# A fused transformer block on one core: statistics of the first band groups in fours, an earlier turn, fewer held banks, later statistics

## The chip, the cores and the metric

The kernel runs on one core of a Trainium2 chip. The metric is device time in microseconds (us), from one launch to its end, as the median of several runs. A core has five engines that run side by side and wait for each other with semaphores: TensorE (PE) for matrix products, VectorE (DVE), ScalarE (ACT), GpSimd (POOL), and SyncE (SP), which here issues most of the transfers between the core's memory (SBUF) and the device memory. PE writes its products into PSUM, which has eight banks of 512 float32 per partition.

## The reference

The input `x` is [2, 256, 128, 128]: batch, time, frequency, channel. All is float32. Three residual parts follow each other:

```python
xt = _ln(x, ln_t_w, ln_t_b).transpose(0, 2, 1, 3)
x = x + _mha(xt, t_wi, t_bi, t_wo, t_bo, H_T, cm).transpose(0, 2, 1, 3)
xf = _ln(x, ln_f_w, ln_f_b)
x = x + _mha(xf, f_wi, f_bi, f_wo, f_bo, H_F, bm)
xn = _ln(x, ln_n_w, ln_n_b)
h = jax.nn.gelu(xn @ w1.T + b1, approximate=False)
x = x + (h @ w2.T + b2)
```

`_ln` subtracts the mean over the channels and divides by the root of the variance plus 1e-5. `_mha` is attention with four heads of 32 channels: over the 256 times with a causal mask `cm` first, then over the 128 frequencies with a mask `bm` that keeps 16 neighbours on each side.

## The kernel before

**Groups.** The work is cut into groups of 512 rows (four tiles of 128). There are 128 groups of attention over time (`OverTime`, groups 0 to 127). Then come 16 runs; each has eight groups of attention over frequencies (`OverBands`) and eight of the feed-forward part (`FeedForward`) on the same rows. The first run's band groups are groups 128 to 135.

**A group's way.** `load` fetches `x`. `statistics` (DVE) takes mean and variance of each row into `mv`: four `bn_stats`, four `bn_aggr`. The reciprocal root of the variance, `rstd`, comes either from `root` on GpSimd (an addition and a power), or from ACT (`root_by_scalar`, logarithm and exponential) with a Newton step of three small DVE instructions (`refine`). `normalize` (DVE) writes `xh`; `turn` transposes blocks of it into `z` (DVE) and sends `z` through device memory with four DMAs into `turned`; `fetch` brings it back transposed as `xnT`. PE then makes queries and keys (`queries_keys`), values (`values`), scores, row sums (`rp`, a product with ones) and weighted values (`op`) in `weigh`. ACT takes the exponentials; GpSimd masks them (`first_mask`), except those of the last band head, to which DVE adds the mask beforehand in PSUM (`by_vector`). ACT's `invert` forms a reciprocal of `rp`; `divide` (DVE) makes three steps: the correction on `rp`, then `u`, then `oT`. `output` (PE) makes `yp`; `finish` (DVE) adds it to the residual and stores it, with four DMAs in every second group. In a feed-forward group PE multiplies by `w1` in four slices (`hidden`), ACT applies GELU, PE multiplies by `w2` (`weigh`), and DVE's `divide` adds the residual.

**The order.** `run` (lines 1111 to 1238) has one loop over steps `n`. Each step does parts of several groups: the scores of group `n`, `weigh` and `divide` of `n-1`, `output` and `finish` of `n-2`, `normalize` and `turn` of `n+3` or `n+4`, queries of `n+1` or `n+2`, statistics further ahead. Every instruction is pinned to the program's order on its engine (`InOrder`), so this loop is the order of each engine's queue, SP's DMAs included; the engines meet only where data or a buffer make one wait.

**Fours.** For groups 12 to 127, four groups share one tile of statistics [128, 16] (`Four`): statistics of group `n+8` in step `n`; after the fourth, `root_in_bank` writes the root of all sixteen columns into a PSUM bank, and one `refine` serves four groups. The first band groups do it alone: `due` places their statistics in steps 123, 124, 124, 125, 127, 128, 129 and 130 and, at the end of the same steps, `root_by_scalar` and `refine`, four columns wide, with the root in SBUF.

**Banks.** In time steps banks have fixed places (`Attention.place`). Elsewhere `turn_of_bank` hands out the eight banks in turn; a bank that comes round again can only be written after its last reader. `OverBands.weigh` takes two turns ahead, `yp` and `qp`, into `held`, for the `output` and `queries_keys` that follow in that step. After the last two band groups of a run no queries follow: one turn is skipped, and the last `qp` is left in `held` and used by the first group of the next run.

"Turn" (in the code, `turn`) is also the name of the first feed-forward step of a run, in which `invert_exactly` uses DVE's reciprocal because ACT has already loaded the table for GELU.

The places that the change touches, in the loop:

```python
do_at(n + 3, (OverBands, FeedForward), "normalize", "turn")
do_at(n + 4, OverTime, "normalize")
if old is not None:
    do(n - 2, "finish")
do_at(n + 4, OverTime, "turn")
...
do_at(n + 5, FeedForward, "statistics")
...
do(n - 1, "weigh")
...
if bands[2] or turn:
    do(n - 2, "output", "finish")
do(n - 1, "divide")
```

All instructions issued through `InOrder` carry one line number in the profile, L926; they are told apart by their tiles. A PSUM tile is always called `bank`.

Of the kernel before, what the change touches and what calls it, by code (L numbers as in the profile page):

```python
# [10 lines left out]
F32 = mybir.dt.float32  # L11
# [8 lines left out]
P = 128  # L20
# [5 lines left out]
NT = 4  # L26
# [399 lines left out]


class Group:

# [22 lines left out]
            vector.bn_aggr(self.mv[:, i, :], stats[:, i, :])  # L454

    def means(self):
        return self.path.small.tile([P, NT, 2], F32, name="mv", bufs=16)

    def root(self):
        path, gpsimd = self.path, self.path.gpsimd  # L460
# [92 lines left out]
    def weigh(self):  # L553
        pass
# [30 lines left out]


class Attention(Group):
    four = None
    which = None
    swapped = ()  # L590
    place = {}
# [77 lines left out]
def rows_of(h):  # L669
    return slice(h * D, (h + 1) * D)  # L670
# [9 lines left out]
class OverTime(Attention):  # L680
# [3 lines left out]
    which = 0  # L684
    swapped = (1, 3)
    early, late = (1, 2), (0, 3)

    def means(self):
        if self.four is None:
            return super().means()  # L690
        if self is self.four.groups[0]:
            self.four.mv = self.path.small.tile([P, NT * NT, 2], F32, name="mvs", bufs=3)
        return self.four.part(self.four.mv, self)

    def values(self):
        path = self.path
# [91 lines left out]
def time_scores(old, new):  # L788


    if new is not None:
        new.first_tiles()
    if old is not None:
        old.second_tiles()
    for kind, h, s, e in TIME_ORDER:
        if kind == "s" and old is not None:
            old.second_scores(int(h), int(s), int(e) * HALF)
        if kind == "f" and new is not None:
            new.first_scores(int(h), int(s), int(e) * HALF)


class OverBands(Attention):


    which = 1
    by_vector = 1

    def scores(self, heads):
# [38 lines left out]
    def weigh(self):  # L847
        path = self.path

        path.held = dict(yp=path.turn_of_bank(), qp=path.turn_of_bank())  # L850
        self.rp = path.bank([P, NT * P], "rp")
        for h in range(H):
            path.tensor.matmul(
                self.rp[rows_of(h), :], path.k.ones[:, 0:D], self.p[:, h].rearrange("p i q -> p (i q)"),
                start=True, stop=True,
            )
        self.op = path.bank([P, NT * P], "op")
        for i in range(NT):
            c = slice(i * P, (i + 1) * P)
            for h in range(H):  # L860
                r = rows_of(h)
                path.tensor.matmul(self.op[r, c], self.v[:, i, r], self.p[:, h, i, :], start=True, stop=True)
# [68 lines left out]
class BoundedPath:  # L931
# [179 lines left out]
    def run(self, x, out):  # L1111
        groups = list(self.groups(x, out))

        def do(n, *names):
            if 0 <= n < len(groups):
                for name in names:
                    getattr(groups[n], name)()

        def at(n, kind):
            return 0 <= n < len(groups) and isinstance(groups[n], kind)  # L1120

        def do_at(n, kind, *names):
            if at(n, kind):
                do(n, *names)


        timed = [g for g in groups if isinstance(g, OverTime)]
        fours = {i + NT - 1: Four(self, timed[i : i + NT]) for i in range(3 * NT, len(timed), NT)}

        run0 = [i for i in range(len(groups)) if at(i, OverBands)][: RUN // NT]  # L1130
        due = dict(zip(run0, (-5, -4, -4, -3, -1, 0, 1, 2)))
        due = {n: [i for i in run0 if run0[0] + due[i] == n] for n in range(-12, len(groups) + 2)}
        A = RUN // NT

        self.scalar.preload_act_table_set(EXP_SET)
        for n in range(-12, len(groups) + 2):
            feeds = [at(n - 2 + i, FeedForward) for i in range(5)]
            bands = [at(n - 2 + i, OverBands) for i in range(5)]
            turn = feeds[2] and bands[1]
            old, new = (groups[i] if at(i, OverTime) else None for i in (n, n + 1))  # L1140
            if bands[2] and feeds[1]:
                self.scalar.preload_act_table_set(EXP_SET)
            do_at(n + 4, FeedForward, "root")
            do(n, "first_half", "first_function", "first_mask")
            if n >= 0:
                if n + 5 < 3 * NT:
                    do(n + 5, "statistics")
                if n >= NT:
                    do_at(n + 2 * NT, OverTime, "statistics")
            if old is not None or new is not None:  # L1150
                time_scores(old, new)
                b = self.banks
                Attention.place = dict(yp=b["b0"], rp=b["b3"], op=b["a1"], qp=b["a2"], kp=b["b1"], vp0=b["b0"], vp1=b["b2"])
            else:
                Attention.place = {}
            if old is not None:
                old.second_weights(old.late)
                do(n - 2, "output")
            if new is not None:
                new.first_weights(new.early[:1])  # L1160
            if old is not None:
                old.second_weights(old.early)
                old.mask_second()
                old.add(0)
                old.add(1)
            if new is not None:
                new.first_weights(new.early[1:])
            if n >= 0:
                if n + 5 < 3 * NT:
                    do(n + 5, "root_in_bank")  # L1170
                if n + 2 * NT in fours:
                    fours[n + 2 * NT].root_in_bank()
            if turn:
                do(n, "second_half", "second_function")
            do_at(n + 3, OverTime, "fetch")
            do_at(n + 2, (OverBands, FeedForward), "fetch")

            for i in (2 * n + 12, 2 * n + 13) if n < 2 else (n + 14,):
                if i >= NT:
                    do(i, "load")  # L1180
            if n < -8:
                do(n + 12, "load")
            if n >= 0:
                for i in due[n]:
                    do(i, "statistics")
            do_at(n + 3, (OverBands, FeedForward), "normalize", "turn")
            do_at(n + 4, OverTime, "normalize")
            if old is not None:
                do(n - 2, "finish")
            do_at(n + 4, OverTime, "turn")  # L1190
            if n >= 0:
                if n + 5 < 3 * NT:
                    do(n + 5, "refine")
                if n + 2 * NT in fours:
                    fours[n + 2 * NT].refine()
            if n < 0:
                do(n + 5, "statistics")
            do_at(n + 5, FeedForward, "statistics")
            if n == -4:
                self.fold_rest()  # L1200
                self.warm()
            do(n - 1, "weigh")
            do(n - 1, "invert_exactly" if turn else "invert")
            if new is not None:
                new.first_weights(new.late)
            if bands[2] or turn:
                do(n - 2, "output", "finish")
            do(n - 1, "divide")
            if not turn:
                do(n, "second_half", "second_function")  # L1210
            if n in run0:
                do(n, "bias")
            if not bands[2] and old is None:
                do_at(n, FeedForward, "bias")
                do_at(n + A, OverBands, "bias")
                if at(n - 1, FeedForward) and at(n - 2, OverBands):
                    do_at(n + A - 1, OverBands, "statistics", "root")
                if not turn:
                    do_at(n + A, OverBands, "statistics", "root")
            do_at(n + 2, OverTime, "queries_keys", "take_query", "take_key")  # L1220
            do_at(n + 1, OverBands, "queries_keys", "take_query", "take_key")
            if n < 0:
                do_at(n + 5, OverTime, "root_by_scalar", "refine")
            for i in due[n]:
                do(i, "root_by_scalar", "refine")
            do_at(n, OverTime, "bias")
            if new is not None:
                new.mask_first()
            if not bands[2] and not turn and old is None:
                do(n - 2, "output", "finish")  # L1230
            do_at(n + 2, OverTime, "values", "take_values")
            do_at(n + 1, OverBands, "values", "take_values")
            if old is not None or new is not None:

                b = self.banks
                self.banks = dict(
                    a1=b["b3"], a2=b["a2"], b0=b["a0"], b3=b["a3"], a0=b["a1"], a3=b["b1"], b1=b["b0"], b2=b["b2"]
                )
# [69 lines left out]
```

## Time and profile before

| | us |
|---|---|
| median of three runs | 2680.13 |
| lowest and highest | 2678.06, 2683.11 |
| profiled execution | 2683.14 |
| its span, first to last instruction | 2681.4 |
| busy: PE, DVE, POOL, ACT | 2638.5, 2146.5, 1950.0, 1844.5 |
| granted PE clock, mean | 0.999 |

The stages in the trace: time groups to about 944 us, then sixteen runs of about 107 us. Busy times in stretches of 50 us show that the engines stand differently in them: from 300 to 350 us PE is busy 50.0 us, DVE 42.3, ACT 45.0, POOL 46.4; from 1300 to 1350, around the band groups of a run, PE 49.2, DVE 49.1, ACT 31.8, POOL 35.7; from 1350 to 1400, mostly feed-forward, PE 50.0, DVE 29.5.

A line of a timeline has the start and length in us, engine, source line, operation, output and input tiles with their shapes, how many such instructions were merged, and, in brackets, how long the engine was idle before and whom it waited for. Ends of PE instructions are modelled, so a busy PE may still be waiting inside a group of matmuls: the distance between the starts of the same product in successive steps tells more.

### The profile page before, as it was taken

Reading aid. Unit: us, or ns where it says so; the run is one execution under the profiler, and the core shown is the slowest. Engines: PE = TensorE matmul, PEld = TensorE weight load, DVE = VectorE, ACT = ScalarE, POOL = GpSimd, SP = SyncE. Lnnn points to the kernel's source line nnn. Section 1 sums busy time; section 2 is a strip of 40 time slices with the busy share of each in tenths; the row PEclk is TensorE's granted clock in tenths of the full one; section 3 lists DMA queues with packets and bytes.
Section 4 is the critical chain, followed back from the end, with each engine's and each line's share of the span. In section 5 each row is a group of like instructions: output and inputs, shape, how many; then the busy total and the mean of one; then the engine's idle time right before and its main releaser. Section 6 shows DMA issues by size and latency. Waiting matters only on the chain.

```text
span 2681.4 us, 156498 instructions
## 1 busy us (share of the span) xinstructions
PE 2638.5 (98%) x68662; PEld 1805.6 (67%) x68662; DVE 2146.5 (80%) x6447; ACT 1844.5 (69%) x3574; POOL 1950.0 (73%) x2297
## 2 busy tenths in 40 slices
PE   7999999999999999999999999999999999999998
PEld 5766666666766666666666666666666677666665
DVE  6888888878888896968868769688687696886874
ACT  6899989889899874664755746647557466475573
POOL 4999999989999986766667657666676576665762
PEclk9999999999999999999999999999999999999999
DMA  6555555555555444545445445444444454544533
GB/s 150 149 160 151 155 150 155 141 145 152 157 149 155 121 122 113 129 113 132 116 115 133 109 120 125 125 126 115 120 129 110 117 132 116 127 116 120 130 95 83
DMA packets 471510, 347.08 MB, mean 129 GB/s; under 512 B 43296, under 2 KB 405152, under 8 KB 470816
## 3 DMA queue, kind: packets, MB, share of 16 engines
q1 hardware_dynamic: 469568, 335.92, 48.5%
q8 instruction: 540, 8.85, 1.4%
q14 instruction: 154, 1.26, 0.2%
q10 hardware_dynamic: 1248, 1.05, 0.2%
HBM read 169.03 MB, written 167.77 MB: 126 GB/s over the span
## 4 chain that ended last, share of the span: by engine, by line
PE 80%; DVE 15%; DMA 2%; issue 1%; ACT 1%; SPq 0%; DVEq 0%; ACTq 0%
PE bank L926 80%; DVE xh L926 4%; DVE bank L926 3%; DVE stats L926 2%; DVE z L926 2%; DVE u L926 2%; DVE x L926 1%; DMA xnT<-turned 1%; DVE mv L926 1%; DMA turned<-z 1%; SPq L926 0%; DVE oT L926 0%; ACT p L926 0%; DVE vy L926 0%; DMA f_wiT_sb<-in_f_wiT 0%
## 5 line engine op out<-in xcount | busy, mean ns | idle before, releaser
L926 ACT ACTIVATE hT<-bank,b 128x512 f32<-128x512 f32 x512 | 347.3, 688 | 535.6 <-PE bank L926 516.9
L926 POOL TENSOR_SCALAR_AFFINE_SELECT pf<-pf 128x512 f32<-128x512 f32 x768 | 478.1, 637 | 246.7 <-ACT pf L926 220.3
L926 PEld LDWEIGHTS bank<-w2T_sb,hT 128*32 128x32 f32 x16384 | 459.7, 110 | 62.1 <-issue 39.2
L926 PE MATMUL bank<-xnT,wf 128*32 128x512 f32 x4096 | 491.2, 594 | 5.5 <-ACT p L926 3.0
L926 PE MATMUL bank<-w2T_sb,hT 128*32 128x128 f32 x16384 | 477.2, 273 | 0.5 <-issue 0.3
L926 PE MATMUL bank<-xnT,w1f 128*32 128x512 f32 x4096 | 475.5, 592 | 0.0
L926 ACT ACTIVATE p<-bank 128x512 f32<-128x512 f32 (+1 forms) x1024 | 430.7, 494 | 64.1 <-PE bank L926 64.0
L926 POOL TENSOR_SCALAR_AFFINE_SELECT p<-p 128x1024 f32<-128x1024 f32 (+2 forms) x384 | 363.2, 946 | 87.1 <-ACT p L926 78.8
L926 DVE TENSOR_SCALAR xh<-x,mv,rstd 128x160 f32<-128x160 f32 x1072 | 417.7, 431 | 10.0
L926 DVE TENSOR_TENSOR res<-bank,res 128x512 f32<-128x512 f32 x256 | 175.6, 686 | 258.9 <-PE bank L926 227.2
L926 PEld LDWEIGHTS bank<-wf,xnT 128*32 128x32 f32 x8192 | 237.3, 110 | 154.0 <-issue 100.6
L926 POOL TENSOR_TENSOR p<-p,p 128x512 f32<-128x512 f32 x256 | 323.8, 1285 | 10.7
L926 DVE BATCH_NORM_STATS2 stats<-x 128x6 f32<-128x128 f32 x1536 | 326.4, 275 | 0.1
L926 PE MATMUL bank<-qT,kT 32*64 32x80 f32 (+4 forms) x16384 | 317.3, 273 | 5.2 <-DVE u L926 1.8
L926 PEld LDWEIGHTS bank<-qT,kT 32*64 32x64 f32 x16384 | 273.4, 131 | 58.3 <-ACT kT L926 47.4
L926 ACT ACTIVATE pf<-bank 128x512 f32<-128x512 f32 x512 | 266.9, 602 | 53.5 <-PE bank L926 50.4
L926 POOL TENSOR_SCALAR rstd<-mv 128x4 f32<-128x4 f32 x248 | 56.8, 229 | 313.0 <-DVE mv L926 311.7
L926 PEld LDWEIGHTS bank<-xnT,w1f 128*32 128x32 f32 x4096 | 155.5, 110 | 191.0 <-issue 167.4
L926 DVE STREAM_TRANSPOSE z<-xh 128x512 f32<-128x512 f32 x384 | 272.0, 708 | 9.1
L926 PE MATMUL bank<-wn,oT 128*32 128x128 f32 x8192 | 275.6, 274 | 0.7 <-DVE oT L926 0.7
L926 PE MATMUL bank<-wf,xnT 128*32 128x128 f32 x8192 | 273.6, 273 | 0.1
L926 POOL TENSOR_TENSOR rstd<-rstd,mhalf 128x4 f32<-128x4 f32 x248 | 256.9, 1036 | 20.7
(102 smaller groups left out, 3775.3 us busy)
## 6 DMA issues: line engine op xcount, KB each, us to landing
turned<-z SPq DMA_DIRECT2D x1536, 64.0 KB, 2.7
xnT<-turned SPq DMA_DIRECT2D x384, 256.0 KB, 3.0
x<-in_x SPq DMA_DIRECT2D x128, 256.0 KB, 4.2
x<-res SPq DMA_DIRECT2D x256, 128.0 KB, 3.3
x<-x SPq DMA_DIRECT2D x128, 256.0 KB, 4.2
out<-res SPq DMA_DIRECT2D x256, 128.0 KB, 2.5
w1T_sb<-in_w1T ACTq DMA_DIRECT2D x1, 256.0 KB, 5.6
w2T_sb<-in_w2T ACTq DMA_DIRECT2D x1, 256.0 KB, 7.8
```

Of the source, the lines that this page charges most:

```text
L926: return self.tc.keep_in_program_order(emit(*args, **kwargs))
```

## The change

Four parts, in one diff:

- The first eight band groups join the scheme of fours: `times` covers groups 12 to 135, their statistics run in steps 120 to 127, and two `Four`s make root and refine in steps 123 and 127. `due` goes, and `means` moves up to `Group`.
- In time steps `turn` of group `n+4` comes before `finish` of `n-2`, on DVE and, with its DMAs, on SP.
- `OverBands.weigh` holds a bank for `qp` only where the group two further on is also a band group.
- In band steps and in the step named `turn`, `statistics` of feed-forward group `n+5` comes after `divide` of `n-1`; in the others it stays.

```diff
 class Group:
+    four = None
...
     def means(self):
-        return self.path.small.tile([P, NT, 2], F32, name="mv", bufs=16)
+        if self.four is None:
+            return self.path.small.tile([P, NT, 2], F32, name="mv", bufs=16)
+        if self is self.four.groups[0]:
+            self.four.mv = self.path.small.tile([P, NT * NT, 2], F32, name="mvs", bufs=3)
+        return self.four.part(self.four.mv, self)
...
 class OverBands(Attention):
     which = 1
+    follow = ("yp",)
     by_vector = 1
...
-        path.held = dict(yp=path.turn_of_bank(), qp=path.turn_of_bank())
+        path.held = {name: path.turn_of_bank() for name in self.follow}
...
-        timed = [g for g in groups if isinstance(g, OverTime)]
-        fours = {i + NT - 1: Four(self, timed[i : i + NT]) for i in range(3 * NT, len(timed), NT)}
+        for i in range(len(groups) - 2):
+            if at(i, OverBands) and at(i + 2, OverBands):
+                groups[i].follow = ("yp", "qp")
 
         run0 = [i for i in range(len(groups)) if at(i, OverBands)][: RUN // NT]
-        due = dict(zip(run0, (-5, -4, -4, -3, -1, 0, 1, 2)))
-        due = {n: [i for i in run0 if run0[0] + due[i] == n] for n in range(-12, len(groups) + 2)}
+        times = range(3 * NT, run0[-1] + 1)
+        fours = {i + NT - 1: Four(self, groups[i : i + NT]) for i in times[::NT]}
...
-                if n >= NT:
-                    do_at(n + 2 * NT, OverTime, "statistics")
+                if n + 2 * NT in times:
+                    do(n + 2 * NT, "statistics")
...
-            if n >= 0:
-                for i in due[n]:
-                    do(i, "statistics")
             do_at(n + 3, (OverBands, FeedForward), "normalize", "turn")
-            do_at(n + 4, OverTime, "normalize")
+            do_at(n + 4, OverTime, "normalize", "turn")
             if old is not None:
                 do(n - 2, "finish")
-            do_at(n + 4, OverTime, "turn")
...
-            do_at(n + 5, FeedForward, "statistics")
+            if not bands[2] and not turn:
+                do_at(n + 5, FeedForward, "statistics")
...
             do(n - 1, "divide")
+            if bands[2] or turn:
+                do_at(n + 5, FeedForward, "statistics")
...
-            for i in due[n]:
-                do(i, "root_by_scalar", "refine")
```

On the engines' queues: PE's and GpSimd's instructions keep their order (only bank numbers differ on PE); DVE has 18 small instructions fewer and ACT 12; SP issues the same transfers, with the stores of a time group after the turned blocks.

More of the change, by code (lines that the diff above doesn't have):

```diff
@@ L587 @@
 class Attention(Group):
-    four = None
     which = None
@@ L686 @@
     early, late = (1, 2), (0, 3)
[L688 to L693, printed above, removed]
     def values(self):
```

## The prediction

> **What bounds the kernel now.** I read the page first, then PE's waits, then the timelines of PE, VectorE (DVE) and GpSimd (POOL) over one late run (1280 to 1395 us), over the change of stage (895 to 1010 us) and around the one long stall (535 to 575 us).
>
> ```profile
> PE 2638.5 (98%) x68662; PEld 1805.6 (67%) x68662; DVE 2146.5 (80%) x6447; ACT 1844.5 (69%) x3574; POOL 1950.0 (73%) x2297
> ```
> ```profile
> PE bank L926 <- DVE u L926: 13.2, 17, 1.8
> PE bank L926 <- ACT p L926: 4.6, 4, 1.8
> PE bank L926 <- DMA xnT<-turned: 2.4, 1, 2.4
> ```
>
> PE is 98% busy, so little can be gained by removing work from others; the gaps count. The waits (us in total, times, longest) show the largest: 17 times PE waits until DVE's `u` has been written. Sixteen runs of band attention and feed-forward, and one at the change of stage.
>
> The same place in one run, PE's timeline (start, length, instruction, idle before):
>
> ```profile
> 1297.83 1.06 PE L926 MATMUL bank<-pf,ones 128*32 128x512 f32 x8
> ...
> 1323.18 1.06 PE L926 MATMUL bank<-pf,ones 128*32 128x512 f32 x8
> ...
> 1325.81 3.62 PE L926 MATMUL bank<-xnT,w1f 128*32 128x512 f32 x32
> 1330.22 1.06 PE L926 MATMUL bank<-pf,ones 128*32 128x512 f32 x8 [0.80 <-DVE u L926]
> ```
>
> The third row sum (`pf,ones`, the product with ones that makes `rp`) starts at 1297.83, the eighth at 1330.22: 32.39 us, and 32.38 to 32.59 in all 15 later runs. Unstalled steps are 6.25 apart; the last interval is 7.04. So 31.24 is PE's floor for the five intervals and 1.15 is lost, 0.80 of it as one gap.
>
> ```profile
> 1317.66 0.69 DVE L926 SCALAR_TENSOR_TENSOR bank<-bank,band 128x512 f32<-128x512 f32 x1
> ...
> 1320.53 0.83 DVE L926 BATCH_NORM_STATS2 stats<-x 128x6 f32<-128x128 f32 x4
> 1321.28 0.36 DVE L926 BATCH_NORM_AGGREGATE mv<-stats 128x2 f32<-128x6 f32 x4
> 1321.56 0.66 DVE L926 TENSOR_TENSOR x<-bank,x 128x512 f32<-128x512 f32 x1
> ...
> 1324.19 0.69 DVE L926 SCALAR_TENSOR_TENSOR bank<-bank,band 128x512 f32<-128x512 f32 x1
> ```
>
> DVE has no idle time here: from one band mask (`bank,band`) to the next it takes 6.53 us ((1324.19 - 1298.08) / 4), 0.28 more than PE needs. In each such step the statistics of a feed-forward group (1.03 us, 1320.53 to 1321.56) stand ahead of `x`, `u` and `oT`, which PE waits for. PE's busy share hides this lag: the score matmuls stretch from 0.92 to 1.06.
>
> GpSimd is nearly as full:
>
> ```profile
> 1321.73 0.23 POOL L926 TENSOR_SCALAR rstd<-mv 128x4 f32<-128x4 f32 x1 [0.21 <-DVE mv L926]
> 1322.04 1.04 POOL L926 TENSOR_TENSOR rstd<-rstd,mhalf 128x4 f32<-128x4 f32 x1
> 1324.00 3.94 POOL L926 TENSOR_SCALAR_AFFINE_SELECT pf<-pf 128x512 f32<-128x512 f32 x6 [0.92 <-ACT pf L926]
> ```
>
> Root (1.31 from start to the next instruction) and masks (3.94) make 5.25 of 6.53 us; the root already waits for DVE's `mv`.
>
> At the change of stage the three refine instructions of a group beside GpSimd, then PE's wait:
>
> ```profile
> 949.93 0.94 DVE L926 SCALAR_TENSOR_TENSOR vy<-mv,root 128x4 f32<-128x4 f32 x1 [0.21 <-ACT root L926]
> 950.91 1.21 DVE L926 SCALAR_TENSOR_TENSOR vy<-vy,root 128x4 f32<-128x4 f32 x1
> 952.15 0.55 DVE L926 SCALAR_TENSOR_TENSOR rstd<-vy,root 128x4 f32<-128x4 f32 x1
> ```
> ```profile
> 958.57 0.35 PE L926 MATMUL bank<-qT,kT 32*64 32x80 f32 x2 [1.78 <-DVE u L926]
> ```
>
> The stall in the time stage, PE's timeline:
>
> ```profile
> 561.42 3.59 PE L926 MATMUL bank<-xnT,wf 128*32 128x512 f32 x16 [2.43 <-DMA xnT<-turned]
> ```
>
> **What the Trainium skill says.** Four places bear on this. GPSIMD Engine Reference, Key points: GpSimd shares its SBUF interfaces with VectorE, and they contend when VectorE is in a two-port mode or reads two SBUF inputs. VectorE: DVE Perf Modes, Why PSUM operands drop a tier: an operand in PSUM rules the two-port mode out. The trace agrees: with the root in SBUF the 4-wide `vy` takes 0.15 to 1.2 us, with the root in a bank the 16-wide one never exceeds 0.173. PSUM — Partial Sum Buffer, PSUM bank collisions raise a hardware error: engines must be kept apart per bank by semaphores, so a bank is not reusable before its last reader is done; here that is the wait on `u`. TensorE: Matmul & The Clock Gate, Part 1: after an idle window of about 3.4 us the clock is halved. At 561.42 the sixteen matmuls after an idle of only 2.43 us take 3.59 instead of 1.90, so the trace shows the penalty after less idle time than the page names.
>
> **The change part by part.**
>
> *Statistics and roots of the first eight band groups.* Statistics (1.03 us each) move from steps 123 to 130 to steps 120 to 127, the slots that time groups used, where steps stay at 7.08 us with the same load. Eight refines (24 DVE instructions, some 11 us in DVE's timeline from 919 to 975, up to 2.7 us each while GpSimd runs) become two of about 0.5 us on PSUM, sixteen small ACT instructions (about 0.5 us a group) become four. Where this reaches PE: the time steps of 7.22, 7.63 and 8.25 us go back to 7.08: 0.14 + 0.55 + 1.17 = 1.86. The 5.66 us step after them waits for ACT's exponentials and `oT` and stays. In the 9.04 us step from 952.86 to 961.90, DVE's refine (2.8 us) and statistics (1.0) leave, so that only PE's `yp` (953.9) holds it: residual 0.6, first division 0.65, `u` 0.7, done at about 955.9 instead of 958.5; PE would then miss its score banks (those of `u` and `oT`) by some 0.1 us: 2.6 saved. The next slow step, 6.83 to 6.25: 0.6. From the third to the eighth row sum this run takes 34.21 us; with the backlog gone it is like the later runs: 34.21 - 32.43 (their mean) = 1.8. Sum 6.9 us.
>
> *Banks.* Without the held `qp`, the eighth row sum no longer lands on the bank of the seventh (which `u` frees) but on that of an earlier `yp`, freed a DVE step before. Alone this removes the 0.80 gap. In exchange the seventh row sum lands on the bank of the sixth group's `op`, freed by its `oT`. Also, before, the first `qp` of a later run takes the left-over bank, and `vp` then the same one: V starts 1.87 us after QK (1382.18 to 1384.05) instead of 1.72. That goes too: 0.16 x 15 = 2.4 us.
>
> *Late statistics.* `x`, `u`, `oT` come 1.03 us earlier, and PE's score banks with them, while the band mask stays where it is in DVE's stream. But `mv` comes 2.63 us later (`x`, the first division, `u`, `oT` go ahead: 1321.56 to 1324.19), and behind the root that waits for it on GpSimd stand the masks of that step, which the row sum needs. The last step: `mv` is ready at about 1324.27, root at 1324.36, masks 1325.67 to 1329.61 (before: 1327.94). The third head's mask is the last; two heads' row sums may go ahead of it, so the eighth row sum effectively starts at about 1329.5. The bank side gives the same: `oT` of the sixth group ends near 1323.24, the seventh row sum starts at 1323.3 and the eighth 6.24 later (2.63 of products, 3.61 of feed-forward), 1329.5. So 1330.22 - 1329.5 = 0.7 saved, not 1.15: the statistics that leave PE's path come back through GpSimd. For 16 runs 11.2 us. Bounds: 1.15 (GpSimd hides it) and nothing.
>
> After that, the turn step: DVE's 3.32 us reciprocal starts 1.03 earlier, so `oT` is ready near 1337.9, PE wants it at 1339.0. No new wait. Feed-forward steps are PE's (6.9 us each, DVE idle 3 us), so the gain is kept.
>
> *Turn ahead of the residual.* In some 120 time steps the transpose (0.65 us to the next instruction) fills DVE's wait for `yp`; the residual ends at most 0.65 us later. PE needs its bank again for V: in the step of 549, residual done 551.2 instead of 550.5, V at 553.44, 2.2 us to spare. Steps are at PE's 7.08, so nothing is gained there. But on SP every second step's four stores (549 to 551.4) stood ahead of the four `turned` DMAs (551.43 to 554.8), and now stand behind. The data of the next projection are turned about 2.5 to 3 us earlier, against a stall of 2.43 us. Behind the stores, which wait for the residual (551.2), now stands the next fetch; with 1.9 us for four issues they are done at 553.1, before the turned data land (`z` 550.6, issue 1.9, landing 2.7: 555.2). It should vanish: 11.42 - 7.08 = 4.34 us of this execution, the slow clock included. Bounds: 0 (another transfer late) and 4.34.
>
> Sum: 6.9 + 2.4 + 11.2 + 4.3 = 24.8 us from this execution's 2683.14 (span 2681.4 and 1.7 around it): 2658.3. The median of the three runs is 2680.13, the lowest 2678.06; 2683.14 less the stall is 2678.8, so I take it that runs differ by such stalls and that the forecast holds for the median without a second deduction. Rounded, 2659.
>
> **Rivals.** (a) GpSimd hides the roots: PE at its floor in each run, 0.45 x 16 = 7 us more, 2651. For: two of three masked heads may go ahead. Against: 5.25 of 6.53 us full, and locked to `mv`. (b) The gap only changes its owner, from `u` to the masks: 11 us less gain, 2670. For: root and masks follow `mv` without slack. Against: the numbers above leave 0.7. (c) The residual's bank: if in time steps the residual ended past V's start (2.2 us later than I reckon), 0.2 us in each of 120 steps, 24 us, would cancel all; at 0.4 it is 2707, slower. Against: DVE idles 0.25 to 0.75 us twice a step. (d) It doesn't do what it says: the lag stays at the change of stage, other stalls take the stores' place: 2676 to 2680, no change.
>
> **How the numbers follow.** Forecast 0.61, (a) 0.14, (b) 0.18, (c) 0.03, (d) 0.04. Faster by over 0.2% (5.4 us, what can be told from no change) 0.93, within it 0.04, slower 0.03. The range goes from (a) to (b): 2650 to 2670.
>
> **What would show it.** No 4-wide `vy` near 920 to 975 and steps of 7.08 us to the end of the time stage; the wait on `u` gone from PE's list; third to eighth row sum 31.7 us (31.24 is (a), 32.4 is (b)); GpSimd's root in band steps waiting for `mv` each time, masks ending near 1.7 us later against DVE; the V of a run's first band group 1.72 us after QK; no PE wait on `xnT`. Wrong would be a time step above 7.08 throughout, or a wait on `res`.

## The result and the profile after

The changed kernel takes 2663.52 us, the median of six runs (2662.45 to 2665.47), where six runs of the kernel before have a median of 2681.93, 18.4 us more: a ratio of 0.9929 with a 95% interval of 0.9914 to 0.9944. The profiled execution took 2662.95 us, its span is 2661.2 and its mean granted clock 0.999, against 2683.14, 2681.4 and 0.999 before. It is faster by about 0.7%, 4.5 us short of the forecast of 2659 and inside its range. In the changed kernel all instructions of `InOrder` carry L924.

The page's first part after (busy time, share of the span, instructions):

```profile
PE 2630.1 (99%) x68662; PEld 1930.4 (73%) x68662; DVE 2140.1 (80%) x6429; ACT 1841.8 (69%) x3562; POOL 1947.3 (73%) x2297
```

PE is busy 8.4 us less, the share goes from 98% to 99%. The work of the other engines is nearly the same, so the 20.2 us of span came from gaps and from PE groups that no longer stretch. Only the weight loads (PEld) are busy for longer, by 124.8 us; the last section comes back to that. The waits of PE (us in total, times, longest):

```profile
PE bank L924 <- ACT p L924: 4.6, 4, 1.8
PE bank L924 <- DVE oT L924: 4.3, 13, 0.7
```

The 17 waits on `u` (13.2 us) are gone from the list. In their place stand 13 on `oT`, 4.3 us: one at the change of stage, the others in 12 of the 16 runs, 0.17 to 0.44 us each. The places are these, in the same late run as before; PE's timeline (start, length, instruction, idle before and whom it waited for):

```profile
1284.35 1.07 PE L924 MATMUL bank<-pf,ones 128*32 128x512 f32 x8
...
1309.98 1.06 PE L924 MATMUL bank<-pf,ones 128*32 128x512 f32 x8 [0.27 <-DVE oT L924]
...
1312.58 3.64 PE L924 MATMUL bank<-xnT,w1f 128*32 128x512 f32 x32
1316.02 1.33 PE L924 MATMUL bank<-pf,ones 128*32 128x512 f32 x8
```

From the third row sum (1284.35) to the eighth (1316.02) it is 31.67 us, before 32.39. The wait before the eighth (0.80 on `u`) is gone, one of 0.27 on `oT` stands before the seventh, and the last interval is 6.04 instead of 7.04. The seventh row sum is written into the bank that the sixth group's `oT` frees, as the prediction had it. DVE's timeline beside it:

```profile
1304.27 0.67 DVE L924 SCALAR_TENSOR_TENSOR bank<-bank,band 128x512 f32<-128x512 f32 x1
...
1308.42 0.69 DVE L924 SCALAR_TENSOR_TENSOR u<-bank,r 128x512 f32<-128x512 f32 x1
1309.14 0.69 DVE L924 TENSOR_TENSOR oT<-bank,u 128x512 f32<-128x512 f32 x1
1309.75 0.86 DVE L924 BATCH_NORM_STATS2 stats<-x 128x6 f32<-128x128 f32 x4
1310.53 0.37 DVE L924 BATCH_NORM_AGGREGATE mv<-stats 128x2 f32<-128x6 f32 x4
1310.81 0.68 DVE L924 SCALAR_TENSOR_TENSOR bank<-bank,band 128x512 f32<-128x512 f32 x1
```

The statistics (1309.75, 1310.53) now stand behind `oT`. From mask to mask DVE still takes 6.54 us (1310.81 - 1304.27), as before; it is only the order inside the step that changed. `oT` ends at 1309.83 and PE starts at 1309.98. GpSimd in the same step:

```profile
1310.98 0.23 POOL L924 TENSOR_SCALAR rstd<-mv 128x4 f32<-128x4 f32 x1 [1.31 <-DVE mv L924]
1311.30 1.04 POOL L924 TENSOR_TENSOR rstd<-rstd,mhalf 128x4 f32<-128x4 f32 x1
1312.31 3.93 POOL L924 TENSOR_SCALAR_AFFINE_SELECT pf<-pf 128x512 f32<-128x512 f32 x6
```

The root now waits 1.31 us for `mv`, and the masks behind it run from 1312.31 to 1316.24. PE's eighth row sum starts at 1316.02, before the last of them is written, and is 1.33 us long where the others are 1.06. Against DVE's mask of the step the masks start 1.50 us late (1312.31 against 1310.81), where before they started 0.19 us early (1324.00 against 1324.19).

At the change of stage the refine is one for four groups, on a root in a bank; DVE's timeline, and PE's score matmuls of that step, after and then before:

```profile
941.20 0.15 DVE L924 SCALAR_TENSOR_TENSOR vy<-mvs,bank 128x16 f32<-128x16 f32 x1
941.39 0.17 DVE L924 SCALAR_TENSOR_TENSOR vy<-vy,bank 128x16 f32<-128x16 f32 x1
941.60 0.17 DVE L924 SCALAR_TENSOR_TENSOR rstds<-vy,bank 128x16 f32<-128x16 f32 x1
```
```profile
943.46 1.41 PE L924 MATMUL bank<-qT,kT 32*64 32x80 f32 x64
```
```profile
949.77 0.97 PE L926 MATMUL bank<-qT,kT 32*64 32x80 f32 x64
```

The three instructions, 16 columns wide, take 0.15 to 0.17 us beside a busy GpSimd; those of the group shown before, 4 columns wide in SBUF, 0.55 to 1.21. This fits what the Trainium skill (VectorE: DVE Perf Modes, Why PSUM operands drop a tier) lets one expect of an operand in PSUM; width and place were not changed one at a time. But they stand, 0.49 us from 941.20 to 941.69, ahead of the division of this step, where no refine stood before. Its `oT` ends at 943.90, and the score matmuls are stretched from 0.97 to 1.41 us.

Between the two profiled executions the 20.2 us come out as follows, from the starts of the same products in both traces. 4.6 up to the end of the undisturbed time steps, 4.34 of which is the stall at 561 us. 6.6 over the change of stage and the first run, up to its eighth row sum. 10.6 over the 15 later runs. Then 1.6 is lost again behind the last run.

### The profile page after: what moved, and what is told of

It is laid out like the page before. It is cut to its first block, busy times and chain, and to the rows that moved or that the text cites. A ratio compares the mean times of both kernels' runs of the same rounds, so it can differ in the third digit from the quotient of the medians.

```text
span 2661.2 us, 156426 instructions
## 1 busy us (share of the span) xinstructions
PE 2630.1 (99%) x68662; PEld 1930.4 (73%) x68662; DVE 2140.1 (80%) x6429; ACT 1841.8 (69%) x3562; POOL 1947.3 (73%) x2297
## 3 DMA queue, kind: packets, MB, share of 16 engines
q10 hardware_dynamic: 1248, 1.05, 0.2%
## 4 chain that ended last, share of the span: by engine, by line
PE 86%; DVE 10%; DMA 2%; SPq 0%; issue 0%; ACT 0%; DVEq 0%; ACTq 0%
PE bank L924 86%; DVE xh L924 2%; DVE bank L924 2%; DVE z L924 1%; DVE u L924 1%; DVE oT L924 1%; DVE stats L924 1%; DVE x L924 1%; DMA xnT<-turned 1%; DMA turned<-z 1%; SPq L924 0%; DVE mv L924 0%; DMA x<-in_x 0%; DMA rows_sb<-in_rows 0%; ACT p L924 0%
## 5 line engine op out<-in xcount | busy, mean ns | idle before, releaser
L924 ACT ACTIVATE hT<-bank,b 128x512 f32<-128x512 f32 x512 | 346.9, 688 | 527.0 <-PE bank L924 496.3
L924 POOL TENSOR_SCALAR_AFFINE_SELECT pf<-pf 128x512 f32<-128x512 f32 x768 | 476.8, 635 | 178.5 <-ACT pf L924 152.2
L924 PEld LDWEIGHTS bank<-w2T_sb,hT 128*32 128x32 f32 x16384 | 498.2, 110 | 22.9 <-issue 16.7
L924 PE MATMUL bank<-xnT,w1f 128*32 128x512 f32 x4096 | 510.0, 592 | 0.0
L924 PE MATMUL bank<-w2T_sb,hT 128*32 128x128 f32 x16384 | 504.0, 273 | 0.2 <-ACT hT L924 0.2
L924 PE MATMUL bank<-xnT,wf 128*32 128x512 f32 x4096 | 492.5, 592 | 3.5 <-ACT p L924 3.0
L924 ACT ACTIVATE p<-bank 128x512 f32<-128x512 f32 (+1 forms) x1024 | 430.4, 495 | 65.0 <-PE bank L924 64.6
L924 POOL TENSOR_SCALAR_AFFINE_SELECT p<-p 128x1024 f32<-128x1024 f32 (+2 forms) x384 | 363.6, 947 | 81.2 <-ACT p L924 72.9
L924 DVE TENSOR_SCALAR xh<-x,mv,rstd 128x160 f32<-128x160 f32 x1040 | 404.4, 431 | 9.7
L924 PEld LDWEIGHTS bank<-wf,xnT 128*32 128x32 f32 x8192 | 243.6, 110 | 144.0 <-issue 103.2
L924 DVE TENSOR_TENSOR res<-bank,res 128x512 f32<-128x512 f32 x256 | 170.5, 666 | 218.8 <-PE bank L924 192.0
L924 PEld LDWEIGHTS bank<-xnT,w1f 128*32 128x32 f32 x4096 | 247.2, 110 | 128.2 <-issue 114.9
L924 POOL TENSOR_TENSOR p<-p,p 128x512 f32<-128x512 f32 x256 | 323.9, 1287 | 10.7
L924 DVE BATCH_NORM_STATS2 stats<-x 128x6 f32<-128x128 f32 x1536 | 329.5, 277 | 0.2 <-DMA x<-in_x 0.2
L924 POOL TENSOR_SCALAR rstd<-mv 128x4 f32<-128x4 f32 x248 | 56.3, 227 | 369.1 <-DVE mv L924 368.3
L924 PE MATMUL bank<-qT,kT 32*64 32x80 f32 (+4 forms) x16384 | 314.3, 273 | 2.4 <-ACT p L924 1.0
L924 PEld LDWEIGHTS bank<-qT,kT 32*64 32x64 f32 x16384 | 271.3, 131 | 54.5 <-ACT kT L924 50.3
L924 ACT ACTIVATE pf<-bank 128x512 f32<-128x512 f32 x512 | 266.7, 602 | 46.7 <-PE bank L924 44.1
L924 PE MATMUL bank<-wn,oT 128*32 128x128 f32 x8192 | 283.4, 274 | 0.7 <-DVE oT L924 0.7
L924 DVE STREAM_TRANSPOSE z<-xh 128x512 f32<-128x512 f32 x384 | 273.3, 712 | 13.2
L924 PE MATMUL bank<-wf,xnT 128*32 128x128 f32 x8192 | 276.7, 273 | 0.0
L924 POOL TENSOR_TENSOR rstd<-rstd,mhalf 128x4 f32<-128x4 f32 x248 | 256.6, 1035 | 20.7
```

The costliest lines, as they stand in the source:

```text
L924: return self.tc.keep_in_program_order(emit(*args, **kwargs))
```

## Experiments

All medians are of four or more runs beside runs of the kernel before on the same chip (2679.95 us for the first group of experiments, 2681.96 for the second, 2680.36 for the third). The first four put one part of the change back, with the other three in place. The changed kernel did not run beside these four; differences are taken to its 2663.52 us. Its second median, beside the next group, is 2664.36, so that a difference of 1 us or less says nothing here.

**Statistics and roots of the first eight groups in their old places** (`u_four`).

```diff
+        due = dict(zip(run0, (-5, -4, -4, -3, -1, 0, 1, 2)))
...
-        times = range(3 * NT, run0[-1] + 1)
+        times = range(3 * NT, run0[0])
...
+            for i in due[n]:
+                do(i, "root_by_scalar", "refine")
```

> The changed kernel with its first part undone (the first eight band groups again make statistics and roots singly in steps 123 to 130). Theory: the change of stage alone was worth 11.21 us to the eighth row sum of the first run, less 4.6 gained before it and 0.7 that every run gains: 5.9. So 2669.4 us (the changed kernel has 2663.5), time steps of 7.6 and 8.2 us again, one of 9.0, a PE wait on u near 950 us, and later runs unchanged at 31.7 us from third to eighth row sum. Rival (the gain at the change of stage is that of the other parts, which also work there): within 1 us of 2663.5.

2669.81 us (2669.11 to 2670.82), ratio 0.9959 (0.9946 to 0.9972): 6.3 us more than the changed kernel. The time steps of 7.21, 7.64 and 8.24 us are back, and PE's list of waits again has, once,

```profile
PE bank L924 <- DVE u L924: 1.8, 1, 1.8
```

The later runs stay at 31.7 us from the third to the eighth row sum. The prediction gave this part 6.9.

**The turn behind the residual again** (`u_turn`).

```diff
-            do_at(n + 4, OverTime, "normalize", "turn")
+            do_at(n + 4, OverTime, "normalize")
             if old is not None:
                 do(n - 2, "finish")
+            do_at(n + 4, OverTime, "turn")
```

> The changed kernel with turn behind finish again in time steps. Theory: no time step changes its 7.08 us, but stalls on xnT return in some executions, each of 2 to 4 us: median 2664 to 2668, spread of 3 us or more where the changed kernel has 3.0. Rival (the stall was chance and the order of SP's queue has no part in it): median and spread as for the changed kernel, 2663.5 within 1.

2663.85 us (2660.59 to 2669.52), ratio 0.994 (0.9925 to 0.9955). The median moves by 0.3, but the lowest and highest are 8.9 us apart, where the changed kernel has 3.0. Its profiled execution happens to have no stall on turned data, and starts better. PE's timeline of the changed kernel near the start has one:

```profile
54.95 2.23 PE L924 MATMUL bank<-xnT,wf 128*32 128x512 f32 x16 [0.56 <-DMA xnT<-turned]
```

This is the fifth projection. Reckoned from the output product before it (51.14), it comes 3.81 us later, 0.56 of it as a wait for `xnT`; here it comes 3.06 later (50.54 to 53.60). Not every execution with the turn ahead has this wait: in that of `u_late` the projection comes 3.06 us later, too. From the first output product to the sixth it takes 36.0 us here and 37.5 in the changed kernel. In the profiled executions of this study the means are 36.4 (three with the turn behind, 36.0 to 36.8) and 37.3 (nine with the turn ahead, 36.4 to 38.1; the tenth, that of `a_hold`, has a gap of 1.42 us there that the trace puts down to no other engine, and is left out). These ranges overlap. What stands apart is the sum of the third to fifth time step, 22.3 us in all nine and 21.9 in all three, so that the turn ahead costs 0.4 us there; the rest of the 0.9 lies in the first step, which varies from 7.1 to 8.7 us. The median doesn't show the 4.3 us that the prediction had entered.

**Both banks held after every band group** (`u_bank`).

```diff
-            if at(i, OverBands) and at(i + 2, OverBands):
+            if at(i, OverBands):
                 groups[i].follow = ("yp", "qp")
```

> The changed kernel that holds both banks in every band group again. Theory: late statistics alone take the gap away, since u is done 1.03 us earlier; the masks then set the eighth row sum, third to eighth 31.7 us as before the undoing; V of a run's first band group starts 1.87 us after QK again, 0.15 x 15 = 2.3 us: 2665.8. Rival (the banks remove the gap): the wait on u is back, 32.4 us, 11 us more, 2675.

2665.64 us (2663.82 to 2666.36), ratio 0.9942 (0.9929 to 0.9954): 2.1 more than the changed kernel, though the two ranges overlap. With the statistics late, the old assignment of banks makes PE wait nowhere in the runs, neither on `u` nor on `oT`. The two sizes expected inside a run missed: the third to eighth row sum takes 31.51 us and not 31.7, and V comes 2.21 us after QK and not 1.87.

**Statistics in their old place ahead of `x`, `u` and `oT`** (`u_late`).

```diff
-            if not bands[2] and not turn:
-                do_at(n + 5, FeedForward, "statistics")
+            do_at(n + 5, FeedForward, "statistics")
...
             do(n - 1, "divide")
-            if bands[2] or turn:
-                do_at(n + 5, FeedForward, "statistics")
```

> The changed kernel with feed-forward statistics in their old place. Theory: the gap moves to the seventh row sum, which lies on the bank that oT of the group before the last frees, 1.03 us later than in the changed kernel: third to eighth row sum 32.4 to 32.6 us, PE waiting on oT for 1.0 to 1.3 us once a run, no wait on the masks: 9 to 13 us more, 2673 to 2676. Rival (the banks remove the gap, late statistics only hold the masks up): 2659 to 2664.

2674.83 us (2673.28 to 2675.74), ratio 0.9976 (0.9968 to 0.9984): 11.3 more. PE's waits, its timeline at the seventh and eighth row sum, and DVE's `oT` beside it:

```profile
PE bank L924 <- DVE oT L924: 18.4, 17, 1.2
```
```profile
1312.14 1.06 PE L924 MATMUL bank<-pf,ones 128*32 128x512 f32 x8 [1.17 <-DVE oT L924]
...
1318.18 1.07 PE L924 MATMUL bank<-pf,ones 128*32 128x512 f32 x8
```
```profile
1311.31 0.69 DVE L924 TENSOR_TENSOR oT<-bank,u 128x512 f32<-128x512 f32 x1
```

The wait on `u` before the eighth row sum is gone, as the prediction said that the banks alone would do; but before the seventh PE now waits 1.17 us for the `oT` that ends at 1312.00. The banks alone move the gap one step ahead and make it longer (18.4 us in 17 waits, against 13.2 before).

**The root on GpSimd behind the masks, a bank skipped once more, and both.** The trace of the changed kernel leaves two things late in a run: GpSimd's masks, behind a root that waits for `mv`, and the seventh row sum's bank. `a_root` moves the root in band steps behind the masks; `a_hold` skips the turn of `qp` only after a run's last group, so that the seventh row sum falls on an earlier bank; `a_both` does both. The changed kernel ran once more beside them (`after_again`).

```diff
-            do_at(n + 4, FeedForward, "root")
+            if not bands[2]:
+                do_at(n + 4, FeedForward, "root")
             do(n, "first_half", "first_function", "first_mask")
+            if bands[2]:
+                do_at(n + 4, FeedForward, "root")
```
```diff
-            if at(i, OverBands) and at(i + 2, OverBands):
+            if at(i, OverBands) and at(i + 1, OverBands):
```

> The changed kernel itself, as the measure for the three beside it: 2663.5 us, third to eighth row sum 31.7 us, first row sum of that stretch 1.06 and the eighth 1.33 us long.

> The changed kernel with GpSimd's root of a feed-forward group behind the masks of the step instead of ahead of them, in band steps. Theory: two limits stand at almost the same place, the masks (through the root that waits for mv) and the bank of the sixth op (freed by oT). Taking the masks away leaves the bank: third to eighth row sum stays 31.6 to 31.7, but the eighth row sum is 1.06 instead of 1.33 us long and the skew of the feed-forward matmuls goes: 0.27 x 16 = 4 us less, 2659. Rival (the masks were the only limit): 31.1 us, 2649. Other rival (the masks don't matter): 2663.5.

> The changed kernel that still skips a bank after the last band group but one (only the last group holds yp alone), so that the seventh row sum no longer lies on the bank of op. Theory: PE's wait on oT goes, but the masks hold the eighth row sum at the same place: 2662.5 to 2664. Rival (the bank was the only limit): 2653 or less.

> Both of these: root behind the masks and a bank skipped after the last band group but one. Theory: both limits gone, PE at its floor between the row sums, 31.0 to 31.2 us from third to eighth, the eighth 1.06 us long: (0.55 + 0.27) x 16 = 13 us less than the changed kernel, 2650. Rival (DVE's 6.53 us a step sets the end in another way, by x or the bank of op): 2657 to 2661.

| kernel | median us | ratio, 95% interval |
|---|---|---|
| `after_again` | 2664.36 | 0.9927 (0.9908 to 0.9945) |
| `a_root` | 2660.46 | 0.9911 (0.9892 to 0.9929) |
| `a_hold` | 2664.01 | 0.9926 (0.9907 to 0.9944) |
| `a_both` | 2655.52 | 0.9895 (0.9876 to 0.9914) |

The root behind the masks is worth 3.9 us; the bank alone 0.4, which can't be told from nothing (`a_hold` has 2663.11 to 2668.19, `after_again` 2663.19 to 2665.45); both 8.8. Each removes one of two limits that lie at almost the same place, and the second shows its worth only with the first gone. In `a_both` GpSimd's and PE's timelines read:

```profile
1309.82 3.94 POOL L924 TENSOR_SCALAR_AFFINE_SELECT pf<-pf 128x512 f32<-128x512 f32 x6 [1.09 <-ACT pf L924]
1313.74 0.23 POOL L924 TENSOR_SCALAR rstd<-mv 128x4 f32<-128x4 f32 x1
```
```profile
1309.00 1.06 PE L924 MATMUL bank<-pf,ones 128*32 128x512 f32 x8
...
1315.06 1.04 PE L924 MATMUL bank<-pf,ones 128*32 128x512 f32 x8
...
1319.38 3.68 PE L924 MATMUL bank<-w2T_sb,hT 128*32 128x128 f32 x128
```

The masks run first. They start 0.36 us ahead of DVE's mask of that step (1310.18), where in the changed kernel they start 1.50 us behind it. The root finds `mv` ready; the eighth row sum is 1.04 us long again. It didn't reach the 2650 that was expected: the third to eighth row sum takes 31.46 us on the mean, and not 31.0 to 31.2. No wait on PE's list accounts for the rest. The score matmuls are 0.99 to 1.12 us long there, and in this run the next row sum starts 0.93 to 1.05 us after them, where the prediction's unstretched step has 0.92. DVE still takes 6.55 us from mask to mask; that this stretches the score matmuls was not tried.

**What a run costs, in all kernels.** From the starts on PE's timeline: the mean over the 15 later runs from the third to the eighth row sum, from there to the first row sum of the next run, the distance of V from QK in a run's first band group, and the mean period of a run (first row sum of the second run to that of the sixteenth, by 14), in us.

| kernel | third to eighth | eighth to next first | V after QK | period |
|---|---|---|---|---|
| before | 32.43 | 63.16 | 1.90 | 107.35 |
| after | 31.71 | 63.18 | 1.72 | 106.65 |
| `after_again` | 31.84 | 63.13 | 1.72 | 106.75 |
| `u_bank` | 31.51 | 63.64 | 2.21 | 106.90 |
| `u_late` | 32.68 | 62.93 | 1.71 | 107.36 |
| `a_hold` | 31.48 | 63.48 | 1.72 | 106.73 |
| `a_root` | 31.72 | 62.98 | 1.72 | 106.47 |
| `a_both` | 31.46 | 62.93 | 1.71 | 106.15 |

Two executions of the changed kernel differ by 0.10 us in the period. The second column alone deceives: `u_bank` and `a_hold` look better than the changed kernel there, and are not better in the period. What they win up to the start of the eighth row sum they lose after it: that row sum waits for its last masks and is 1.54 and 1.55 us long on the mean, where the changed kernel has 1.33. Only where the masks come in time (`u_late`, `a_root`, `a_both`) is the next stretch 62.9 to 63.0.

**The turn ahead alone, and kept out of the first steps.** `b_turn` is the kernel before with this part of the change only. `a_three` is `a_both` with the turn behind the residual in the first eight steps. `a_both` ran again beside them.

```diff
-            do_at(n + 4, OverTime, "normalize", "turn")
+            do_at(n + 4, OverTime, "normalize")
+            if n >= 8:
+                do_at(n + 4, OverTime, "turn")
             if old is not None:
                 do(n - 2, "finish")
+            if n < 8:
+                do_at(n + 4, OverTime, "turn")
```

> The kernel before with the turn ahead of the residual as its only change. The prediction's step: the stall on the turned data (4.34 us of the profiled execution) goes; it took that for the median, too. Theory now (after the run with the turn put back, whose median did not move): stalls on the turned data come in some executions only, so that the turn ahead draws in the spread and not the median; the first time step costs about 0.7 us more. So: median within 2 us of the kernel before, the span between lowest and highest about 2 to 5 us where the kernel before has 10 or more, and no wait on xnT after the first 60 us. Rival (the prediction's step holds for the median): 3 to 5 us less than before. Second rival (the narrow spread of the changed kernel comes from its other parts): spread like that of the kernel before.

> The fastest version so far (root behind the masks in band steps, the bank skipped after the last-but-one band group too) with the turn behind the residual in the first eight steps alone. If the turn ahead lengthens the first time steps (7.4 to 8.4 us for the first, 7.5 for the fourth and fifth, where they are 7.1 and 7.36 with the turn behind), it takes 0.7 to 1.5 us off that version: about 2654.5. Rival (these steps are taken up by a later wait or vary by chance): the same time as that version, within 0.5 us.

> The fastest version so far once more, on the same chip as the two others: 2655.5, 8 to 9 us less than the changed kernel.

`b_turn`: 2679.49 us, ratio 0.9995 (0.9986 to 1.0003). The median is 0.9 less, no difference that can be told; its 13 runs lie within 4.3 us (2677.89 to 2682.19), the 17 of the kernel before within 10.7 (2677.32 to 2688.04). Its longest wait on turned data is

```profile
PE bank L926 <- DMA xnT<-turned: 1.0, 1, 1.0
```

near the start, as in the changed kernel. `a_three`: 2654.00 us (2652.38 to 2654.87), ratio 0.9904 (0.9889 to 0.9919), against 2655.73 of `a_both` on the same chip (2652.78 to 2656.24). Its fourth and fifth time steps are 7.38 us long instead of 7.50 to 7.51, as expected; the first, 7.80, lies between those of the two executions of `a_both` (7.41 and 8.72). It is the fastest by its median; since the two ranges overlap, how much of the 1.7 us belongs to the first steps is not settled.

## Why the prediction held, and which term did not

The mechanisms were as predicted, and so were most sizes. Of the 24.8 us of the sum the profiled executions show 20.2. The 4.6 that are missing: 2.3 in the later runs (15 times 0.7 + 0.16 was said, 10.6 found), 1.0 at the change of stage and in the first run (6.9 + 0.7 said, 6.6 found), 1.6 behind the last run, which the sum didn't have, less 0.3 that came more at the start. Point by point:

- *Change of stage, 6.9.* 6.3 by `u_four`. In the trace the steps of 7.63 and 8.25 us are 7.08; the step of 7.22 kept its 7.22, which leaves 1.72 of 1.86. The 9.04 us step became 6.60 (2.44 of 2.6). What the prediction left out is the step before: with a refine ahead of its division it takes 9.44 instead of 9.00 us (9.00 again in `u_four`).
- *Late statistics and banks in the runs, 11.2.* The third to eighth row sum takes 31.71 us where 31.7 was said, between the bounds 31.24 and 32.4; the root waits for `mv`, the masks come 1.69 us later against DVE than before (1.7 was said), and a wait on `oT` stands before the seventh row sum in 12 of the 16 runs. That the sum met 31.7 is in part luck, for two of its terms were off and cancelled. The seventh row sum starts 25.68 us after the third on the mean, where 25.47 was said (1323.3 - 1297.83). The eighth starts 6.03 to 6.04 us after the seventh in all later runs, where 6.24 was said: the feed-forward product was entered with 3.61 us, near its modelled length, while the next product starts 3.44 after it (1316.02 - 1312.58). PE's floor for the five intervals is then nearer 31.04 (4 x 6.25 + 6.04) than 31.24. So the masks don't set the start of the eighth row sum, which follows the seventh and its bank; they only lengthen it (with the masks in time, `a_root` has 31.72, too). "That the statistics come back through GpSimd" is shown by `a_root`: with the root behind the masks the time falls by 3.9 us. That it was a double limit, of bank and of masks, is shown by `a_hold` and `a_both`.
- *"Alone this removes the 0.80 gap."* It does and gains nothing: `u_late`'s period is 107.36, that of before 107.35. The banks lose 0.25 us a run at the seventh row sum and win 0.23 behind the run. They are worth something (0.15 to 0.25 us a run by `u_bank`, against the two executions of the changed kernel) only with the statistics late; the statistics alone bring 0.45 (107.35 - 106.90), both 0.70.
- *V after QK, 2.4.* The distance is 1.72 in all 15 runs, as said, yet the next run starts no sooner: 63.18 against 63.16. The 0.27 us by which the eighth row sum is longer took its place: it comes out at the scores that follow V (last section). Here the step "two heads' row sums may go ahead of it, so the eighth row sum effectively starts at about 1329.5" failed: heads that go ahead hide the wait for the masks from the start that is read, and don't remove it. `u_late`, where the masks are in time, does have the 0.23 us.
- *The stall, 4.3.* This is the term that was sized wrongly for the median. In the profiled execution it is gone, with 4.34 us. But "the forecast holds for the median without a second deduction" did not: `u_turn` and `b_turn` give 0.3 and 0.9. The kernel before seems to stall in some executions, which its spread suggests (one stalled execution was profiled), and to remove that costs something in every one: 0.4 to some 0.9 us in the first steps, and 1.4 at the end of the span (below). With the old statistics of the first band groups it seems to cost something at the change of stage, too: the step of 9.04 us takes 10.67 in `u_four` and 11.19 in `b_turn`, one profiled execution of each.

Of the rivals, (a), GpSimd hiding the roots, falls with the waits of the root and the long eighth row sum; (b), the gap changing its owner, is true in kind only: what the new owners keep is 0.17 to 0.44 us before the seventh row sum and 0.27 inside the eighth; (c), the residual's bank, never showed: time steps are 7.08; (d) falls with the result.

## What to carry to other kernels

When work is moved off the late engine's path, ask of each consumer what it waits for next: here GpSimd's masks held the eighth row sum 0.27 us longer than a bank did; the masks' delay removed alone was worth 3.9 us, the bank alone nothing that can be told, both together 8.8. Measure such a change by the period of a whole run and not by the start of one product, for a product of several independent parts starts with its first operand and ends with its last. And take a stall seen in one profiled execution into a forecast of the median only if the spread of the runs says that most of them have it.

## What was not expected of the hardware

A late operand of one part of a product is carried on for a long time. After the long row sum, PE's timeline of the changed kernel shows the groups that follow cut up:

```profile
1318.62 0.63 PE L924 MATMUL bank<-xnT,w1f 128*32 128x512 f32 x2
1318.71 0.39 PE L924 MATMUL bank<-wn,oT 128*32 128x128 f32 x4
1318.92 1.89 PE L924 MATMUL bank<-xnT,w1f 128*32 128x512 f32 x14
```

The first matmuls of the next product start before the last of the one before. I read this as some of the four groups of 32 columns (128*32 in the lines) running behind the others. The split lines go on for some 48 us, to 1366.26 in the feed-forward part. In `a_both`, where the eighth row sum is not stretched, the same products are whole groups, of 16, 32 and 128 matmuls. The Trainium skill (TensorEngine Tiling (Array Packing), Tiling Modes) says that tiles operate independently; the trace fits that, and adds that a lag of 0.27 us between them doesn't close by itself in 48 us of such matmuls. It comes out at the next run's first band group, between V and the scores; the changed kernel, then the kernel before:

```profile
1369.70 1.35 PE L924 MATMUL bank<-wf,xnT 128*32 128x128 f32 x32
1370.97 1.07 PE L924 MATMUL bank<-qT,kT 32*64 32x80 f32 x64
```
```profile
1384.05 1.08 PE L926 MATMUL bank<-wf,xnT 128*32 128x128 f32 x32
1385.06 1.06 PE L926 MATMUL bank<-qT,kT 32*64 32x80 f32 x64
```

From V to the scores it is 1.27 us instead of 1.01, on the mean of the 15 runs as well, and 1.00 in `a_both`; up to V both kernels take the same time from the eighth row sum, but for the 0.18 us of V after QK. In `u_bank`, with 0.48 us of lag, V itself comes late, 2.21 us after QK instead of 1.72. PEld's busy time goes with the lag: 1906.5 to 1931.1 us in the four executions whose eighth row sum is mostly 1.33 us long (`after`, `after_again`, `u_four`, `u_turn`), 1780.1 to 1806.1 in those where it is about 1.06, 1835.7 and 1839.5 in `u_bank` and `a_hold`.

With the turn ahead of the residual the span ends later behind the last residual: its start lies 8.8 to 9.4 us before the end in eleven profiled executions of kernels with the turn ahead in most or all time steps, and 7.5 to 7.6 in the two without (the kernel before and `u_turn`). Behind the data of the last stores the profile shows two fetches of instructions (8 KB each, queue q14) some 2 us apart in each of the eleven, and one in the two. So the end may hang on where the program's last instructions lie and not on its work. Why the order of time steps 1700 us earlier should matter for that is open.
